# Second layer of a two-layer metaformer: taps summed on VectorE or GpSimd, gates spread by four row tiles, experts by halves in one bank

## The chip, the cores and the metric

The kernel runs on one core of one Trainium2 chip, in one launch. The metric is the device time of that launch in microseconds (us), shown as the median of several runs. A profiled execution gives the span from its first to its last instruction, and this span lies a little below the time of the same run.

## What is computed

All arrays are float32. The input `x` holds 8 images of 128 channels and 32x32 positions, so 1024 tokens of 128 channels for each image. The first layer (softmax attention along rows of the image, then a spectral convolution over the tokens) isn't touched by the change. The second layer is, and this is it, cut to what matters:

```python
# x = x + deformable convolution of the normalised x
offset, mask = conv(x, off_w) + off_b, sigmoid(conv(x, mask_w) + mask_b)
for j in range(3):                                   # three taps in a row of the image
    samp = gather(iy0, ix0) * (1 - wy) * (1 - wx) + ...   # four corners of each sample
    out = out + einsum('bhwc,oc->bohw', samp * mask[:, j][..., None], conv_w[:, :, 0, j])
x = x + out + conv_b
# t = t + mixture of experts of the layer-normalised t: 8 experts, the best two of each token
router_probs = softmax(x @ router_w + router_b)
top_p, top_i = top_k(router_probs, 2); top_p = top_p / sum(top_p)
expert_out = einsum('bnd,edc->bnec', x, expert_w) + expert_b
t = t + einsum('bnk,bnkc->bnc', top_p, take_along_axis(expert_out, top_i))
```

The kernel applies the weights of a tap before the gather, so that the three taps of a token are only scaled and added up after it.

## The kernel before

**Order of the program.** Layer one runs first: attention, then the spectral part, which ends in an inverse transform that is done image by image inside the second layer. The second layer is `DeformAndExperts`. `image` writes down for one image a list of operations, each with an engine (or a choice of two), an assumed cost in us, the operations it follows, and the rooms (buffers) that it takes and gives back. `Plan.order` runs through all 8 lists at once as a small clocked model with these costs and with ranks that favour the earlier image, and emits the instructions in the order in which the model starts them. On the chip each engine works strictly through its own part of that order, and semaphores carry the dependences. An assumed cost therefore changes only the order of the instructions and, where an operation has a choice, its engine.

**One image in the second layer.** `lags` and `waves` (lines 2041 to 2056) build the output of layer one in a PSUM bank named `po`, for even and odd tokens in turn; `take_x2` (L1107) copies it out. `back` and `sum_up` (L1134) turn it to token-major layout, `tok`. A normalisation (`norm`, prefix a) follows, then `channels` (L1073 turns it back), then `mixed` (L1201: 8 matmuls that apply the three taps' weights and the offset and mask filters). The results go to tables in HBM (`write`, L1163 and L1167, issued by SyncE), and GpSimd issues 24 gathers for the image (`fetch`, L1244: 8 tiles of 128 tokens by 3 taps). The landed corners are scaled on ScalarE (L1251) or GpSimd (L1257) and folded on VectorE (`fold`, L1266 and L1267) into `sm`, one partial sum for each tap.

`join_taps` (L1272) then adds up the three taps of four tiles on TensorE: three matmuls of `sm` against the identity, 512 columns each, into one bank. `take_x3` (L1281) adds the bank to `tok` on VectorE, which makes `x3`, the input of the expert part. A second `norm` (prefix b) follows for the whole image; where its argument `edge` is true (first norm of the first image, second norm of the last) the Newton steps of the inverse root may run on VectorE in place of GpSimd. `tokens` (L1073) turns the result to channel-major `tc`.

**Gates and experts.** `gates` makes for each token 8 numbers, six of them zero, and writes them into `padded`, in which two tiles of tokens share one 128-column block (64 columns each). Four transposes (L1541) and a copy (L1548) give `gt`: gates on the partitions, two groups of 64 rows. For each of 8 experts then: `spread` (L1357) copies the expert's gate to all 128 partitions by two matmuls of 64 rows and 512 columns, into two banks `pg`; `gate` (L1365) multiplies 1024 tokens by it on VectorE; `expert` (L1373) does two matmuls of 512 columns into two banks `pe`, where the 8 experts add up. `leave` (L1380 and L1385) adds the bias and `x3`, `take_out` copies, and SyncE stores. There is one pair of banks `pg`, and each spread follows the expert before it, across images too: spread, gate, expert, spread form one chain. Other work of TensorE may be placed between a spread and its expert. PSUM has 8 banks of 512 floats per partition: `po` 2, `pt` 2 (all transposes and small results), `pg` 2, `pe` 2.

## Time and profile before

| quantity | value |
| --- | --- |
| median of 4 runs | 1926.96 us (1924.81 to 1936.13) |
| the profiled execution's own time | 1927.2 us |
| its span | 1925.5 us |
| busy TensorE / VectorE / ScalarE / GpSimd | 1728.8 / 1354.8 / 1075.4 / 1135.6 us |
| second layer, from its first matmul to the end | 1346.4 to 1925.5 us |
| first and last gather issued | 1400.5 and 1822 us |
| first spread of image 0 | 1508.8 us |
| gates of 1024 tokens, L1365 | 64 times, 1221 ns on average |
| tap sums on VectorE, L1281 | 16 times, 689 ns on average |

"Busy" is the time in which an engine has an instruction in work. A float32 matmul of the program appears as two matmul records, each with its own weight load, so the count of records is twice that of the matmuls, and since matmuls are pipelined, the duration of a record is longer than the time after which the next one can start. The time from the start of one group to the start of the next is the better price.

### The profile page before, as it was taken

The page shows a single profiled execution, that of the slowest core. Times are in us where ns is not written, and L with a number is a line of the kernel's source. Part 1 is how long each engine was busy: PE and PEld are TensorE (multiplying, and loading weights), DVE is VectorE, ACT ScalarE, POOL GpSimd, SP SyncE. Part 2 cuts the span into 40 slices and gives each one's busy share as a digit, 9 for nine tenths or more (in the row PEclk, how much of TensorE's full clock was granted, in tenths as well). Part 3 has the DMA queues.
Part 4 walks back from the last instruction along what each step waited for, and adds up shares of the span by engine and source line. Part 5 has one row for each costly group of instructions (what it writes and reads, how often), then busy time and mean ns, then how long its engine had stood idle before and what let it go on. Part 6 is the DMA issues. An engine that isn't in the chain of part 4 may idle for free.

```text
span 1925.5 us, 50111 instructions
## 1 busy us (share of the span) xinstructions
PE 1728.8 (90%) x21452; PEld 1002.6 (52%) x21452; DVE 1354.8 (70%) x2073; ACT 1075.4 (56%) x1724; POOL 1135.6 (59%) x1194
## 2 busy tenths in 40 slices
PE   6899999999999999997577899998976989789876
PEld 3455555555555555554233788887754435343332
DVE  3588788888888888887456666665267878778752
ACT  3667667676767666663335455553246667565610
POOL 3678777777878777784330444443067776667700
PEclk9999999999999999999799999999998899889999
DMA  1000000000000000000877122213598856466500
GB/s 29 13 2 23 2 2 23 2 24 2 24 1 24 2 23 2 2 13 2 188 192 236 53 64 69 68 49 125 151 278 270 240 153 185 145 177 189 159 11 22
DMA packets 157959, 156.03 MB, mean 81 GB/s; under 512 B 15408, under 2 KB 136832, under 8 KB 156320
## 3 DMA queue, kind: packets, MB, share of 16 engines
q1 hardware_dynamic: 142368, 102.41, 18.7%
q0 software_dynamic: 15360, 50.34, 8.4%
q8 instruction: 170, 2.79, 0.6%
q14 instruction: 61, 0.50, 0.1%
HBM read 96.39 MB, written 56.33 MB: 79 GB/s over the span
## 4 chain that ended last, share of the span: by engine, by line
PE 70%; DVE 7%; issue 6%; POOL 5%; ACT 5%; DMA 2%; SPq 1%; ACTq 0%; POOLq 0%; DVEq 0%
PE s L603 14%; PE av L655 12%; PE p_g L1891 6%; PE z L624 6%; PE p_out L1373 5%; PE p_z L1940 5%; PE rb L638 3%; PE p_g L1357 3%; DVE ga L1365 2%; PE p_mix L1201 2%; PE p_x L1272 2%; ACT e L608 2%; PE po L2056 2%; PE pq L558 2%; PE pk L572 2%
## 5 line engine op out<-in xcount | busy, mean ns | idle before, releaser
L617 POOL TENSOR_TENSOR t<-e 128x1024 f32<-128x1024 f32 x256 | 607.8, 2374 | 208.4 <-ACT e L608 208.1
L645 DVE TENSOR_TENSOR e<-e,rb 128x2048 f32<-128x2048 f32 x256 | 570.4, 2278 | 85.4 <-PE rb L638 85.4
L608 ACT ACTIVATE e<-s 128x2048 f32<-128x2048 f32 x256 | 480.9, 1878 | 257.0 <-PE s L603 254.5
L603 PE MATMUL s<-q,k 32*128 32x256 f32 x4096 | 296.9, 404 | 14.4 <-ACT e L608 13.5
L655 PE MATMUL av<-e,vt 128*32 128x256 f32 x4096 | 288.2, 389 | 4.0 <-DVE e L645 2.7
L1244 POOL DMA_INDIRECT g<-tab,idx x192 | 194.1, 1011 | 147.3 <-DMA tab<-hx 70.8
L603 PEld LDWEIGHTS s<-q,k 32*128 32x128 f32 x4096 | 187.0, 186 | 138.7 <-ACT e L608 116.7
L1251 ACT ACTIVATE g<-g,w 128x128 f32<-128x128 f32 x612 | 187.5, 390 | 44.3 <-DMA g<-tab,idx 41.1
L1916 POOL TENSOR_SCALAR at<-uc 128x256 f32<-128x256 f32 (+2 forms) x62 | 75.2, 1215 | 173.6 <-PE p_z L1940 118.7
L655 PEld LDWEIGHTS av<-e,vt 128*32 128x32 f32 x4096 | 101.4, 109 | 141.6 <-issue 84.7
L1891 PE MATMUL p_g<-v,a 32*128 32x128 f32 x4096 | 159.3, 284 | 9.4 <-ACT ga L1623 3.7
L1373 PE MATMUL p_out<-ga,ew 128*128 128x512 f32 x256 | 129.7, 631 | 39.3 <-DVE ga L1365 39.2
L631 DVE RECIPROCAL r<-z 128x256 f32<-128x256 f32 x64 | 112.5, 1757 | 73.4 <-PE z L624 73.2
L1891 PEld LDWEIGHTS p_g<-v,a 32*128 32x128 f32 x4096 | 132.3, 186 | 38.3 <-issue 23.0
L1365 DVE TENSOR_TENSOR ga<-p_g,tc 128x1024 f32<-128x1024 f32 x64 | 78.2, 1221 | 76.0 <-PE p_g L1357 75.9
L624 PE MATMUL z<-t,group 128*32 128x256 f32 x2048 | 122.3, 379 | 0.0
L1625 DVE COPY gb<-p_g 128x512 f32<-128x512 f32 x128 | 82.4, 685 | 46.7 <-PE p_g L1891 46.1
L1625 DVE COPY ga<-p_g 128x512 f32<-128x512 f32 x128 | 82.4, 685 | 44.1 <-PE p_g L1891 44.1
L1623 ACT COPY gb<-p_g 128x512 f32<-128x512 f32 x128 | 68.7, 589 | 69.7 <-PE p_g L1891 68.9
L1623 ACT COPY ga<-p_g 128x512 f32<-128x512 f32 x128 | 68.7, 589 | 66.7 <-PE p_g L1891 66.7
L1373 PEld LDWEIGHTS p_out<-ga,ew 128*128 128x128 f32 x256 | 47.1, 197 | 97.2 <-DVE ga L1365 53.3
L624 PEld LDWEIGHTS z<-t,group 128*32 128x32 f32 x2048 | 66.4, 110 | 44.1 <-issue 0.3
(310 smaller groups left out, 2363.8 us busy)
## 6 DMA issues: line engine op xcount, KB each, us to landing
tab<-hx SPq DMA_DIRECT2D x24, 512.0 KB, 4.6
tab<-hx SPq DMA_DIRECT2D x72, 128.0 KB, 4.7
ud<-us SPq DMA_DIRECT2D x8, 1024.0 KB, 5.3
uc<-ud SPq DMA_DIRECT2D x16, 512.0 KB, 4.1
yd<-zs SPq DMA_DIRECT2D x32, 256.0 KB, 3.3
ga<-yd SPq DMA_DIRECT2D x32, 256.0 KB, 6.3
xc<-in_x SPq DMA_DIRECT2D x8, 512.0 KB, 3.9
x1d<-xt SPq DMA_DIRECT2D x8, 512.0 KB, 2.8
```

The source lines that it names most:

```text
L603: nc.tensor.matmul(s[:, j, c, :], img["k"][rows, hg, 2 * r + c, :], q[rows, qc * QU : (qc + 1) * QU], start=True, stop=True,)
L608: nc.scalar.activation(e.rearrange("p j c q -> p (j c q)"), s.rearrange("p j c q -> p (j c q)"), AF.Exp, scale=float(HD) ** -0.5,)
L617: nc.gpsimd.tensor_add(t, e[:, :, 0, :], e[:, :, 1, :])
L624: nc.tensor.matmul(un["z"][32 * j : 32 * j + 32, 0:QU], group, un["t", r][:, j, :], start=(r == 0), stop=(r == 3), skip_group_check=True,)
L645: nc.vector.tensor_tensor(e, e, un["rb"].unsqueeze(2).to_broadcast([P, NH, 2, QU]), ALU.mult)
L655: nc.tensor.matmul(qrt["av"][32 * j : 32 * j + 32, 0:QU], img["v"][:, 2 * r + c, P * hg + 32 * j : P * hg + 32 * j + 32], un["e", r][:, j, ...
L1244: nc.gpsimd.indirect_dma_start(out=t["g", i][:, tap].rearrange("p k c -> p (k c)"), out_offset=None, in_=rows, in_offset=bass.IndirectOffs ...
L1251: nc.scalar.activation(t["g", i][:, tap, k, :], t["g", i][:, tap, k, :], AF.Identity, scale=t["w"][:, i, tap, k : k + 1],)
L1373: nc.tensor.matmul(t["out"][:, j, :], self.ew[:, e, :], t["xg", e][:, 512 * j : 512 * j + 512], start=(e == 0), stop=False, skip_group_che ...
L1623: self.nc.scalar.copy(dst, src)
L1625: self.nc.vector.tensor_copy(dst, src)
L1891: nc.tensor.matmul(banks[j][:, i * P : (i + 1) * P], self.a[rows, 4 * n + i, :], self.v[rows, ch].rearrange("p f k -> p (f k)"), start=Tru ...
```

## The change

Five things change in the second layer; the two layers compute the same function as before.

- **Taps.** `join_taps` and its three matmuls go. `take_x3` adds the three taps of `sm` and `tok` by three additions of 512 elements, on VectorE or on GpSimd, as the planner places them.
- **Gates.** `padded` gives each of the 8 tiles 32 columns, four tiles to a block of 128, so there are two transposes for an image and `gt` is half as wide. `own`, `eb` and their setup go from two groups of 64 rows to four of 32.
- **Spread and gate.** One `spread` now does four experts for half an image: 16 matmuls of 32 rows and 128 columns, whose four row groups write to four different banks. `gate` multiplies 2048 elements at once. The room `pg` is four banks, `po` one bank in place of two.
- **Experts.** For each half of an image, two groups of four matmuls of 512 columns add up in one bank `pe`. `leave` (now 8 matmuls of 128 columns) comes after the first of the two groups.
- **Last image.** Its second norm and its gates run in two halves. Apart from that the planner's assumed costs change (the transposes from 0.6 to 1.1, `mixed` from 0.55 to 0.85, and others).

```diff
-        "sm": 2, "x3": 3, "tt": 1, "tc": 2, "gate": 2, "xg": 3, "ot": 2,
-        "po": 2, "pt": 2, "pg": 1, "pe": 1,
+        "sm": 2, "x3": 3, "tt": 1, "tc": 2, "gate": 2, "xg": 2, "ot": 2,
+        "po": 1, "pt": 2, "pg": 1, "pe": 1,
...
-        for j in range(2):
+        for q in range(4):
             nc.gpsimd.affine_select(
-                out=self.own, in_=self.own, pattern=[[-1, NE], [0, C]], base=-64 * j,
+                out=self.own, in_=self.own, pattern=[[-1, NE], [0, C]], base=-32 * q,
...
-        for j in range(2):
-            nc.sync.dma_start(self.eb[64 * j : 64 * j + NE, :], expert_b)
+        for q in range(4):
+            nc.sync.dma_start(self.eb[32 * q : 32 * q + NE, q, :], expert_b)
...
     def banks(self, tag, name):
-        return self.ps.tile([P, 2, 512], F32, tag=tag, name=name, bufs=self.ROOMS[tag])
+        return self.ps.tile([P, 4, 512], F32, tag=tag, name=name, bufs=self.ROOMS[tag])
...
+    def norm(self, add, prefix, src, dst, eps, ready, take, parts, edge):
+        if parts == 1:
+            return self.norm_part(add, prefix, src, dst, eps, ready, take, range(NT), edge)
+        first = self.norm_part(
+            add, prefix + "0", src, dst, eps, ready[:1], take, range(0, NT // 2), edge
+        )
+        return first + self.norm_part(
+            add, prefix + "1", src, dst, eps, ready[1:], (), range(NT // 2, NT), edge
+        )
...
-        def join_taps(half):
-            t["px", half] = self.bank("pt", "p_x")
-            for tap in range(TAPS):
-                nc.tensor.matmul(
-                    t["px", half], self.ident, t["sm", half][:, :, tap, :],
-                    start=(tap == 0), stop=(tap == TAPS - 1),
-                )
-        def take_x3(half):
+        def take_x3(half, engine):
...
-            nc.vector.tensor_tensor(
-                flat(t["x3"][:, cols, :]), t["px", half], flat(t["tok"][:, cols, :]), ALU.add
-            )
+            x, sm = t["x3"][:, cols, :], t["sm", half]
+            engine.tensor_tensor(x, sm[:, :, 0], sm[:, :, 1], ALU.add)
+            engine.tensor_tensor(x, x, sm[:, :, 2], ALU.add)
+            engine.tensor_tensor(x, x, t["tok"][:, cols, :], ALU.add)
...
-                q = add(
-                    "PE", 1.9, partial(join_taps, half), [q],
-                    take=("pt",) if half else ("pt", "x3"), give=("sm",),
-                )
                 ready.append(
-                    add("DVE", 0.7, partial(take_x3, half), [q, biased] + ready,
-                        give=("pt", "tok") if half else ("pt",))
+                    add({
+                        "DVE": (2.0, partial(take_x3, half, nc.vector)),
+                        "POOL": (3.5, partial(take_x3, half, nc.gpsimd)),
+                    }, 0, None, [q, biased] + ready, take=() if half else ("x3",),
+                        give=("sm", "tok") if half else ("sm",))
                 )
...
-            ("tt",), b == B - 1,
+            ("tt",), 2 if b == B - 1 else 1, b == B - 1,
...
+        gates = self.gates(add, t, tc, b, 2 if b == B - 1 else 1)
+        def spread(half, first):
+            t["pg"] = self.banks("pg", "p_g")
+            for e in range(4):
+                for q in range(4):
+                    rows = slice(32 * q, 32 * q + 32)
+                    nc.tensor.matmul(
+                        t["pg"][:, q, e * P : (e + 1) * P], self.own[rows, first + e, :],
+                        t["gt"][rows, half, :], start=True, stop=True, skip_group_check=True,
+                    )
+        def gate(half):
...
+            nc.vector.tensor_tensor(
+                t["xg"], t["pg"].rearrange("p q (e n) -> p e q n", e=4),
+                x.unsqueeze(1).to_broadcast([P, 4, 4, P]), ALU.mult,
+            )
+        def experts(half, first):
...
+            for e in range(4):
                 nc.tensor.matmul(
+                    t["out"], self.ew[:, first + e, :], xg[:, e, :],
+                    start=(first + e == 0), stop=(first + e == NE - 1), skip_group_check=True,
+                )
+        def leave(half):
+            for q in range(4):
+                out = t["out"][:, q * P : (q + 1) * P]
                 nc.tensor.matmul(
+                    out, self.eb[:, q, :], t["gt"][:, half, :],
+                    start=False, stop=False, skip_group_check=True,
+                )
                 nc.tensor.matmul(
+                    out, t["x3"][:, half * 4 + q, :], self.ident,
+                    start=False, stop=False, skip_group_check=True,
                 )
...
         for half in range(2):
+            done = []
+            for first in (0, 4):
+                end = half == 1 and first == 4
+                p = add(
+                    "PE", 1.1, partial(spread, half, first), [gates[half], tc[half]] + n,
+                    take=("pg",),
+                )
+                p = add(
+                    "DVE", 2.4, partial(gate, half), [p] + e, take=("xg",),
+                    give=("pg", "tc") if end else ("pg",),
+                )
+                e = [p]
+                q = add(
+                    "PE", 3.8, partial(experts, half, first), [p] + done,
+                    take=() if first else ("pe",), give=("xg",),
+                )
+                done = n = [q]
+                if first == 0:
+                    done = [add(
+                        "PE", 2.1, partial(leave, half), done, give=("x3", "gate") if half else (),
+                    )]
+            q = add(copied(take_out, half), 0, None, [q], take=("ot",), give=("pe",))
...
+    def gates(self, add, t, tc, b, parts):
+        if parts == 1:
+            return self.gates_part(add, t, tc, b, range(NT), "", ("gate",)) * 2
+        half = NT // 2
+        return (
+            self.gates_part(add, t, tc[:1], b, range(0, half), "0", ("gate",))
+            + self.gates_part(add, t, tc[1:], b, range(half, NT), "1", ())
+        )
```

## The prediction

> **What bounds the kernel now.** The change touches only the second layer, so I first cut that layer into three stages with the view that gives each engine's busy time by stretch: A up to the first spread of image 0, B up to the first spread of image 6, C the rest. Columns: stretch, length, busy us of TensorE, weight loads, VectorE, ScalarE, GpSimd, then clock, DMA share, GB/s.
>
> ```profile
> 1338.00:1508.80 170.80, 132.34 (x597) 90.88 (x588) 95.65 (x323) 80.21 (x221) 82.70 (x123) 0.90 0.81 246
> 1508.80:1837.40 328.60, 290.92 (x1003) 136.91 (x1002) 255.48 (x610) 200.53 (x603) 224.64 (x321) 0.96 0.57 169
> 1837.40:1925.50 88.10, 64.66 (x202) 25.46 (x202) 31.57 (x72) 7.25 (x16) 0.00 (x0) 0.97 0.05 17
> ```
>
> In B, TensorE is busy 291 of 329 us (89%), VectorE 78%, GpSimd 68% (with the 0.30 us that it stands after nearly every gather, 143 gathers, some 267 us or 81%). In A the DMA queues carry the load. In C no engine is full, so I read its order of time, TensorE and VectorE:
>
> ```profile
> 1890.42 1.13 PE L1357 MATMUL p_g<-gt,ga 64*128 64x512 f32 x4
> 1892.88 1.98 PE L1373 MATMUL p_out<-ga,ew 128*128 128x512 f32 x4 [1.33 <-DVE ga L1365]
> 1894.80 1.13 PE L1357 MATMUL p_g<-gt,ga 64*128 64x512 f32 x4
> ...
> 1891.60 1.23 DVE L1365 TENSOR_TENSOR ga<-p_g,tc 128x1024 f32<-128x1024 f32 x1 [3.15 <-PE p_g L1357]
> ```
>
> Spread, gate and expert take turns: 1890.42 to 1891.60 to 1892.88 to 1894.80, that is 1.18 + 1.28 + 1.92 = 4.37 us for an expert, and each engine waits for the other. Last, the groups that the change removes, and the rows nearest to what it adds:
>
> ```profile
> L1357 PE MATMUL p_g<-gt,ga 64*128 64x512 f32 x256 | 74.3, 658 | 1.2 <-ACT gt L1548 1.2
> L1272 PE MATMUL p_x<-sm,ident 128*128 128x512 f32 x96 | 47.7, 635 | 3.0 <-DVE tok L1134 1.6 <-ACT hx L1209 1.2
> 1061.97 1.32 PE L1891 MATMUL p_g<-v,a 32*128 32x128 f32 x32 [0.46 <-ACT ga L1623]
> L1281 DVE TENSOR_TENSOR x<-p_x,tok x16: 680/691/692, 1445.8 to 1845.7; 128x512 f32<-128x512 f32 x16
> L1267 DVE TENSOR_TENSOR sm<-g x64: 557/558/5391, 1423.1 to 1840.7; 128x384 f32<-128x384 f32 x64
> 1822.81 5.02 POOL L1257 TENSOR_TENSOR g<-g,w 128x512 f32<-128x512 f32 x5
> 1822.86 5.39 DVE L1267 TENSOR_TENSOR sm<-g 128x384 f32<-128x384 f32 x1
> ```
>
> (Durations with slashes are least/median/greatest ns.) L1891, in layer one, already runs 16 matmuls of 32 rows and 128 columns, 32 records, in 1.32 us: four row groups do overlap. The last two lines matter for the rivals.
>
> **Prices on TensorE**, from start to start. A 512-column matmul: two records at 0.43 = 0.86 us (the weight loads of L1373 follow each other at 0.43). A spread pair: 1.05. A burst as L1891: 1.1 (1.32 less the run-out of the last record). Four 128-column matmuls (L1385): 1.09. One 64-row bias matmul (L1380): 1.05.
> - Spread: 64 pairs x 1.05 = 67.2 become 32 bursts x 1.1 = 35.2: -32.0.
> - Taps: 48 x 0.86 = 41.3 go: -41.3.
> - Experts: 128 matmuls either way: 0.
> - `leave`: per half 1.05 + 1.09 = 2.14 becomes 8 x 0.273 = 2.18: +0.6 over 16 halves. Gate transposes 32 to 16: -4.4.
> Sum -77 us of some 474 that these prices give for the layer before.
>
> **Prices on VectorE.** The new adds have two SBUF operands, 512 elements. From L1267 (384: 0.557) and L1266 (768: 0.95), 512 cost 0.69. The instruction order of the changed kernel puts all 16 `take_x3` on VectorE, none on GpSimd: 48 x 0.69 = 33.1 in place of 11.0, +22. The gate: 512 elements from PSUM 0.69, 1024 1.224, so 2048 are 2.29; 32 x 2.29 = 73.3 against 78.2: -5. The two-part last image repeats about 20 small instructions at 0.2, +4; fewer copies and biases fall to VectorE (`hc` 5 to 2, bias 6 to 4, `gt` 5 to 2), about -8. Sum +13. GpSimd gets 4 more multiplies at 1.05 and 2 more bias adds at 2.36: +9.
>
> **Off the path.** Two more affine selects (1.09 each) stand before the first gather, where GpSimd is idle for 67.7 us; two more 4 KB loads on SyncE at 998 us, over 500 us before use. Uncovered they would be 3 us.
>
> **Stage A.** By the order, the 8 `mixed` of image 0, whose tables release the gathers, no longer alternate with the waves of image 2: TensorE work ahead of them falls from 46.6 to 35.6 us at the prices above. Against that, `po` is one bank: a `lags` of the other parity must wait for `take_x2` (1.07 us, about 1.4 with both hand-overs), three times before the tables, +4. So -7; ends -11 (copies hidden) and +6 (the DMA, at 0.81 of its time, sets A anyway, and later copies wait on ScalarE behind its scaling). I take -6.
>
> **Stage B.** Between the same two spreads the order holds 287 us of TensorE work before and 243 after. VectorE goes from 255 to about 266 (13 adds of 2.07 for 12 of 0.69, less 4 of gates and 4 of copies), GpSimd with gaps from 267 to 276. The gain ends where one of the others fills up. If the fullest engine can be used as TensorE is now (0.885): TensorE 247/0.885 = 279, VectorE 266/0.885 = 301, GpSimd 276/0.885 = 312. So -50, -28 or -17. I take -28, VectorE: each spread hands over to it and back, and it now also holds the adds, while GpSimd's gathers can run ahead as far as the four `g` rooms let them. Behind a waiting gate stand folds and statistics, and for the folds wait the `g` rooms and so the gathers.
>
> **Stage C.** A step of four experts for half an image: 1.4 (burst and hand-over) + 2.34 + 3.63 (two pairs: 1.91 + 1.72) = 7.37. Eight steps 59.0 against 16 x 4.37 = 69.9: -10.9; the taps in it -2.6; four `leave` +0.2. Before, transposes (2.2) and router matmuls (1.9) stood in gaps of 1.28 and showed by 1.5; in gaps of 2.34 they hide: -1.5. But the last image's choices of gates in halves (27 small ops and a copy, 7.8 us) stand on VectorE ahead of one gate and TensorE covers 5.0: +2.8. Sum -12. It may be more: before, image 6's gates came late by the 5.39 us fold above; now its first gate follows the last adds directly. Ends -5 and -20; I take -13.
>
> **Sum** against the profiled execution: 1927.2 (span 1925.5, 1.7 around it) - 6 - 28 - 13 = 1880. That execution lies 0.2 us above the median of 1926.96, so no correction.
>
> **A rule that speaks against the change.** The rows first: the add that goes, L1281, reads PSUM and never took over 692 ns in 16 times; folds with both operands in SBUF took up to 5391, in the one case shown exactly while GpSimd did five multiplies in a row. The three new adds are all of the second kind. On average L1267 and L1266 lie 0.10 and 0.08 above their medians, so 48 adds pay 5 us, which the range covers. The Trainium skill, "SBUF — State Buffer", section "SBUF: two separate sides", says the same as a rule: VectorE and GpSimd share one pair of ports as an exclusive lock, held for the whole instruction, and a VectorE instruction with two SBUF inputs needs it against a GpSimd one that reads SBUF. By that rule alone an add that meets one multiply waits about 1 us; an estimate from it, all 48 meeting one, would be some 50 us, and no gain.
>
> **Rivals.**
> 1. *TensorE stays the bound* and the others give way: A -9, B -42 (its 44 us of work less 2 of longer uncovered gates), C -16: 1860. For it: nearly all `spread` to `experts` gaps in B hold 1.4 us or more of other work. Against it: VectorE then stands at 266/287 = 93%.
> 2. *The gathers set B.* GpSimd stands after most gathers, and between the images it waited 6.0 and 8.7 us for statistics. Then B gives 0 to -17, with C -13 and A 0: 1897 to 1914, say 1906.
> 3. *Slower: the adds meet GpSimd.* Place: `take_x3` in A and B, in front of gates. Price: 48 x s for a mean stall s. At s = 0.98 the 47 us are eaten; at 1.5, 1927 - 47 + 72 = 1952. For it: the 5.39 us row. Against it: median folds take 558 ns, so most don't meet.
> 4. *The row groups don't overlap in this place.* 16 x 0.273 = 4.4 for a burst, +3.3 x 32 = 105: 1985. L1891 speaks against it.
>
> **Numbers.** Chances: forecast 0.50, rival 1 0.22, rival 2 0.18, rival 3 0.08, rival 4 0.02. The time is the forecast's, 1880; its own parts give 1927 - (9 + 42 + 20) = 1856 and, with 6, -10 and -5, 1918. As a range I take 1853 to 1908, which leaves out rivals 3 and 4, the worse half of rival 2 and a little of rival 1. A measurement of this kernel tells 0.5% (10 us) from no change. Faster 0.87, same 0.04 (the end of rival 2 and mild stalls of rival 3), slower 0.09.
>
> **What would show it.** Right: no matmul reads `sm`; the new spreads take 1.1 to 1.4 us in 32 records; the gate about 2.29 us; in the last stage a gate every 7.4 us, or 9.6 where a `leave` stands between; VectorE over 85% busy between the first spreads of images 0 and 6, in about 300 us. Wrong: adds far above 0.69 us, above all beside GpSimd multiplies (rival 3); that stage above 320 us with GpSimd full (rival 2) or below 290 (rival 1); the first gather after 1400 us.

## The result, and the profile after

| | before | after |
| --- | --- | --- |
| median of the comparison | 1927.45 us (63 runs) | 1923.58 us (42 runs) |
| ratio, 95% interval | | 0.9976 [0.9968, 0.9984] |
| span of the profiled execution | 1925.5 us | 1921.0 us |
| first matmul of layer two to first spread (A) | 162.4 us | 149.2 us |
| to the first spread of image 6 (B) | 328.6 us | 343.6 us |
| to the end (C) | 88.1 us | 83.1 us |
| first and last gather issued | 1400.5, 1821.8 us | 1394.4, 1825.8 us |

A starts here at the first `po` matmul (1346.4 before, 1345.1 after); B ends and C starts at the first spread of image 6, the last image but one. The kernel is faster by 4 us, not by 47: the sign was right and the size far off. A gained 13 us and B lost 15; A and B together took 491.0 us before and take 492.8 now. C gained 5. So the sign comes from C and from an earlier start of the layer by 1.3 us; stage B, which was to bring 28 of the 47, went the other way.

The same view of the three stages, after (stretch, length, busy us of TensorE, weight loads, VectorE, ScalarE and GpSimd, granted clock, DMA share, GB/s; in lines of the profile PE is TensorE, PEld its weight loads, DVE VectorE, ACT ScalarE, POOL GpSimd and SP SyncE):

```profile
1345.10:1494.30 149.20, 119.27 (x436) 80.94 (x436) 84.98 (x286) 70.94 (x193) 77.11 (x113) 0.86 0.77 231
1494.30:1837.90 343.60, 269.46 (x1623) 166.71 (x1622) 287.98 (x670) 210.68 (x626) 250.80 (x337) 0.85 0.58 175
1837.90:1921.00 83.10, 57.99 (x398) 32.67 (x398) 32.31 (x77) 4.87 (x12) 0.00 (x0) 0.84 0.04 13
```

TensorE's busy time in B fell by 21 us though the list of work fell by 44; its clock fell from 0.96 to 0.85. VectorE is at 84%, no engine is full. The durations that the forecast rested on came out nearly as priced (the gate at 2.28 for 2.29 us, the adds at 0.69 to 0.82 for 0.69), in the groups of VectorE:

```profile
L1378 DVE TENSOR_TENSOR ga<-p_g,tc 128x2048 f32<-128x2048 f32 x32 | 73.1, 2283 | 53.7 <-PE p_g L1369 53.7
L1294 DVE TENSOR_TENSOR x<-x,sm 128x512 f32<-128x512 f32 x16 | 13.1, 816 | 0.5
L1293 DVE TENSOR_TENSOR x<-sm 128x512 f32<-128x512 f32 x16 | 12.1, 758 | 0.3
L1295 DVE TENSOR_TENSOR x<-x,tok 128x512 f32<-128x512 f32 x16 | 11.1, 692 | 0.5
```

**The stretch of the gathers.** B begins and ends at spreads. GpSimd's own stretch, from the first gather to the last, reads otherwise, first before, then after:

```profile
1400.50:1822.80 422.30, 359.50 (x1250) 183.03 (x1250) 321.07 (x837) 259.57 (x782) 302.32 (x438) 0.94 0.67 201
1394.40:1826.80 432.40, 338.03 (x1857) 213.85 (x1856) 346.83 (x854) 264.22 (x784) 321.11 (x444) 0.85 0.65 197
```

GpSimd is busy for 302 us before, and gaps of at most 0.30 us ahead of its instructions (longer ones counted as 0.30) add 76: 90% of 422. After it is 321 + 74, or 91% of 432. Counted the same way, TensorE goes from 88% to 81% and VectorE from 84% to 86%. GpSimd's work grew by 19 us where the forecast had 9; 8.5 of them are the same 192 gathers, which take longer (line, engine, operation, count, busy us, mean ns, idle time before them), one line of each kernel:

```profile
L1244 POOL DMA_INDIRECT g<-tab,idx x192 | 194.1, 1011 | 147.3 <-DMA tab<-hx 70.8 <-issue 48.4 <-DVE sm L1267 8.4
```

```profile
L1263 POOL DMA_INDIRECT g<-tab,idx x192 | 202.6, 1055 | 94.5 <-issue 48.2 <-DMA tab<-hx 15.6 <-DVE a_st L1019 12.5
```

The chain of waits, asked for that stretch (1394 to 1826 us), gives shares by engine and line. Before:

```profile
by line: PE p_out L1373 16.6%; PE p_g L1357 9.4%; PE p_x L1272 7.0%; PE p_mix L1201 6.9%; DMA g<-tab,idx 6.4%; issue 5.8%; DVE ga L1365 4.5%; POOL g L1244 3.8%; PE po L2056 3.2%; DVE g L1266 2.9%; SPq L1167 2.3%; ACT tt L1035 2.2%; PE p_l L
```

After:

```profile
by line: POOL g L1263 13.8%; issue 10.8%; DMA g<-tab,idx 7.9%; DVE g L1285 5.7%; DVE ga L1378 4.4%; PE p_out L1388 4.0%; ACT g L1270 3.5%; POOL g L1276 3.2%; PE p_mix L1220 3.2%; ACT ht L1052 2.2%; DVE sm L1286 1.8%; ACT tt L1052 1.5%; DVE 
```

Added up over all its pieces, TensorE had 233 of the 432 us of this chain before and has 53 now; VectorE went from 60 to 136, GpSimd from 41 to 114. The change did take TensorE off most of the chain, and two engines that were nearly as full took its place at the same length. Whether either of them sets that length the chain alone doesn't show; the experiments ask.

**Stage C.** TensorE, in order of time (start, duration, group, idle time before it and what ended it), and the clock in the same stretch:

```profile
1871.08 1.17 PE L1369 MATMUL p_g<-gt,ga 32*128 32x128 f32 x32
1874.67 5.15 PE L1388 MATMUL p_out<-ga,ew 128*128 128x512 f32 x8 [2.41 <-DVE ga L1378]
1879.75 1.17 PE L1369 MATMUL p_g<-gt,ga 32*128 32x128 f32 x32
1883.43 5.37 PE L1388 MATMUL p_out<-ga,ew 128*128 128x512 f32 x8 [2.51 <-DVE ga L1378]
...
1903.10 3.67 PE L1388 MATMUL p_out<-ga,ew 128*128 128x512 f32 x8 [2.50 <-DVE ga L1378]
```

```profile
1867.40:1874.20 6.80, 4.86 (x53) 3.50 (x51) 1.88 (x1) 0.00 (x0) 0.00 (x0) 1.00 0.00 0
1874.20:1877.60 3.40, 2.93 (x4) 1.38 (x5) 0.42 (x1) 0.00 (x0) 0.00 (x0) 0.50 0.00 0
1877.60:1884.50 6.90, 4.39 (x40) 2.28 (x40) 2.29 (x1) 0.58 (x1) 0.00 (x0) 0.99 0.10 38
1884.50:1887.90 3.40, 3.40 (x6) 1.34 (x5) 0.00 (x0) 0.00 (x0) 0.00 (x0) 0.51 0.00 0
```

The spread takes 1.17 us in 32 records, as forecast. But the step is 1879.75 - 1871.08 = 8.67 us, not 7.37: after most of the gaps at a gate the clock is granted at half for 3.4 us, just when four experts run. Of the eight groups of the stage six take 5.2 to 5.8 us in place of 3.63. Two stay near the forecast: one that had other work before it, and the one at 1903.10, after a gap of 2.50 us like the others.

What tells that gap from the others is its place. All changes of the granted clock in the traces of this case lie on one grid of 3.41 us. Two steps of that grid with the clock at full (TensorE, weight loads and VectorE busy, then the clock):

```profile
1870.80:1874.21 3.41, 1.46 (x36) 1.14 (x34) 1.89 (x1) 0.00 (x0) 0.00 (x0) 1.00 0.00 0
1901.52:1904.93 3.41, 1.83 (x5) 0.90 (x6) 1.44 (x1) 0.00 (x0) 0.00 (x0) 1.00 0.05 19
```

In the first TensorE stood for 1.95 us, and the next step had half the clock; in the second the end of a gap that began in the step before left 1.58 us, and the clock stayed. Over the second layer in all 20 traces, 319 of the 320 full-clock steps in which TensorE stood for 2.0 us or more were followed by half clock, and 28 of some 1750 in which it stood for less than 1.0 us; between the two it was mixed.

### The profile page after: what moved, and what is told of

Its sections match the earlier page's. It is cut to its first block, busy times and chain, and to the rows that moved or that the text cites. A ratio compares the mean times of both kernels' runs of the same rounds, so it can differ in the third digit from the quotient of the medians.

```text
span 1921.0 us, 51642 instructions
## 1 busy us (share of the span) xinstructions
PE 1689.6 (88%) x22204; PEld 1031.3 (54%) x22204; DVE 1378.7 (72%) x2102; ACT 1074.5 (56%) x1716; POOL 1158.4 (60%) x1202
## 4 chain that ended last, share of the span: by engine, by line
PE 59%; DVE 11%; POOL 9%; issue 7%; ACT 5%; DMA 3%; SPq 2%; POOLq 0%; DVEq 0%; ACTq 0%
PE s L603 14%; PE av L655 12%; PE p_g L1926 6%; PE z L624 6%; PE p_z L1975 5%; PE rb L638 3%; POOL g L1263 3%; PE p_out L1388 3%; DVE ga L1378 2%; DMA g<-tab,idx 2%; ACT e L608 2%; PE pk L572 2%; PE pq L558 2%; DVE g L1285 1%; DVE zs L1987 1%
## 5 line engine op out<-in xcount | busy, mean ns | idle before, releaser
L1263 POOL DMA_INDIRECT g<-tab,idx x192 | 202.6, 1055 | 94.5 <-issue 48.2
L1388 PE MATMUL p_out<-ga,ew 128*128 128x512 f32 x256 | 144.3, 716 | 50.9 <-DVE ga L1378 49.2
L1388 PEld LDWEIGHTS p_out<-ga,ew 128*128 128x128 f32 x256 | 56.7, 231 | 122.1 <-issue 82.7
L1378 DVE TENSOR_TENSOR ga<-p_g,tc 128x2048 f32<-128x2048 f32 x32 | 73.1, 2283 | 53.7 <-PE p_g L1369 53.7
```

Source lines behind the costliest of these rows:

```text
L1263: nc.gpsimd.indirect_dma_start(out=t["g", i][:, tap].rearrange("p k c -> p (k c)"), out_offset=None, in_=rows, in_offset=bass.IndirectOffs ...
L1388: nc.tensor.matmul(t["out"], self.ew[:, first + e, :], xg[:, e, :], start=(first + e == 0), stop=(first + e == NE - 1), skip_group_check=True,
```

## The experiments

Three theories were set against each other for B: (1) the chain of spread, gate and experts on TensorE and VectorE, with its cold clock; (2) VectorE is full; (3) GpSimd's gathers set the pace. Four batches fell on chips on which the kernel before takes 1951 to 1952 us, and the last on one like the first (1924 us). Only runs of one kind of chip are compared with each other; ratios are to the kernel before on the same chip. A + B and C are from one profiled execution of each run, and its time can lie off the median: it was 4.8 us under it in r_after, 4.4 under in a_gate and 13.3 under in a_fetch, 6.1 over in e3_taps_only. Differences of A + B or B below some 10 us are therefore no more than hints.

| run | median us | ratio [95%] | A + B | C |
| --- | --- | --- | --- | --- |
| r_before | 1952.3 | 0.9999 [0.9982, 1.0016] | 518.1 | 88.1 |
| r_after | 1972.5 | 1.0117 [1.0077, 1.0157] | 537.5 | 85.4 |
| e1_warm_tail | 1958.8 | 1.0046 [1.0021, 1.0071] | 534.0 | 74.3 |
| e1_warm_all | 1964.2 | 1.0065 [1.0043, 1.0088] | 545.5 | 75.2 |
| e2_taps_back | 1994.3 | 1.0220 [1.0181, 1.0259] | 568.4 | 81.7 |
| e3_taps_only | 1963.0 | 1.0057 [1.0035, 1.0078] | 527.0 | 93.6 |
| e4_two_experts | 1971.4 | 1.0097 [1.0068, 1.0127] | 541.3 | 85.6 |
| a_experts | 1934.0 | 0.9933 [0.9904, 0.9963] | 518.7 | 71.0 |
| a_gate | 1943.9 | 0.9961 [0.9945, 0.9976] | 523.0 | 69.9 |
| a_adds | 1966.4 | 1.0082 [1.0051, 1.0113] | 533.2 | 83.7 |
| a_fetch | 1925.0 | 0.9874 [0.9845, 0.9903] | 496.4 | 72.0 |
| e5_ahead | 1928.2 | 0.9889 [0.9857, 0.9921] | 521.2 | 61.3 |
| e6_one_room | 1943.4 | 0.9964 [0.9939, 0.9989] | 524.2 | 73.0 |
| e7_before_po1 | 1953.0 | 1.0008 [0.9989, 1.0026] | 516.8 | 88.6 |
| e8_old_costs | 1974.6 | 1.0118 [1.0077, 1.0160] | 546.7 | 83.2 |
| e9_cold_cost | 1978.3 | 1.0139 [1.0097, 1.0180] | 550.6 | 78.5 |
| e10_scale_act (chip like the first) | 1907.0 | 0.9903 [0.9885, 0.9921] | 482.6 | 80.1 |
| e11_ahead_act (chip like the first) | 1907.7 | 0.9898 [0.9880, 0.9916] | 495.9 | 65.2 |

### The two kernels on the other chips

> The changed kernel as it is, beside the three that follow, so that they are compared on one chip. As profiled before: stage A (first matmul of layer two to the first spread) 149 us, stage B (to the first spread of the last image) 344 us, stage C (to the end) 83 us.

> The kernel before as it is, for its stages on these chips, where it takes 1951 us and the changed kernel 1972 us (A 153.3, B 384.2, C 85.4). On the chip of the first comparison it had A 162.4, B 328.6, C 88.1. If the 22 us by which the changed kernel is slower here lie in the late signals of TensorE that its trace shows from the first gather on, B of before is about 353 and its trace shows fewer such delays; if they lie in the change itself, A and C differ as well.

No edit. Here the changed kernel is slower than before by 1.2%. B grew from 352.6 to 384.2 us (+32, where the first chip had +15); A (165.5 to 153.3) and C (88.1 to 85.4) moved about as on the first chip. These traces show what the first chip's don't, TensorE's signals arriving late (start, duration, engine, group, idle time before and its end, where "remote" and "issue" mean that the profile names no sender; r_after):

```profile
1569.12 1.17 PE L1369 MATMUL p_g<-gt,ga 32*128 32x128 f32 x32
1570.22 1.65 PE L1220 MATMUL p_mix<-gw,hc 128*128 128x411 f32 x4
1577.93 2.29 DVE L1378 TENSOR_TENSOR ga<-p_g,tc 128x2048 f32<-128x2048 f32 x1 [5.51 <-remote]
1578.02 0.91 ACT L1228 COPY hx<-p_mix 128x411 f32<-128x411 f32 x2 [6.64 <-issue]
```

The spread is recorded as done at 1570.3, and both the gate and the copy of another matmul's result start together 7.6 us later. Of 15 gates between 1490 and 1840 us before which VectorE was idle, 10 came more than half a microsecond after the end of their spread, some 50 us in all; on the first chip it was none of 9. The expectation for r_before held on B (353) but not on the signals: summed from the end of a matmul that should signal to the next signal seen, its trace has 123 us of such time and r_after's 130. The late signals burden both kernels; how much of the 32 us is theirs is not told apart. Nor does the trace tell whether the signal or the matmul itself was late.

The two stages B, r_before and then r_after:

```profile
1512.20:1864.80 352.60, 300.79 (x1001) 139.43 (x1000) 249.97 (x610) 201.02 (x603) 222.89 (x321) 0.92 0.54 157
```

```profile
1496.40:1880.60 384.20, 284.00 (x1623) 172.54 (x1622) 282.81 (x672) 209.07 (x623) 247.17 (x333) 0.82 0.53 157
```

TensorE is busy for 17 us less, VectorE for 33 and GpSimd for 24 more, and no engine passes 74% in the second: the stage is longer without a fuller engine.

### The clock

```diff
         def experts(half, first):
+            for _ in range(2 if b >= B - 2 else 0):
+                nc.tensor.matmul(
+                    t["out"], self.idle, self.ew[:, 0:4, :].rearrange("p e c -> p (e c)"),
+                    start=(first == 0), stop=False, skip_group_check=True,
+                )
             for e in range(4):
```

`idle` holds zeros, so the two matmuls add nothing; they fill the gap at the gate. e1_warm_all has `True` as its condition.

> The changed kernel, and for the last two images two more matmuls of 512 columns with a zero stationary ahead of each group of four experts (they add zero to the output bank); the order of all other instructions is unchanged. Theory (clock): in the changed kernel TensorE stands 2.4 us in each gate of the last stage, the granted clock falls to half again and again (0.84 on average from the first spread of image 6 on, 0.97 before the change), and four experts take 5.2 us in place of 3.6. The two matmuls (1.7 us warm) fill the wait: clock of the last stage to 0.95 or more, experts near 3.6 us, the last stage from 83 to about 73 us, the whole 8 to 10 us below the changed kernel. Rival (the serial hand-over alone costs the time): clock as before or without effect, last stage 83 us or longer by what of the two matmuls does not fit in the wait.

> The same two zero matmuls ahead of every group of four experts, all images. Theory (clock): the middle stage too loses some 40 us to half clock (0.85 on average over 344 us); with the fillers its clock rises towards 0.95, it shortens by 10 to 25 us although TensorE gets 24 x 1.7 = 41 us of extra work, most of it in waits; whole 15 to 35 us below the changed kernel. Rival (VectorE and the order of the program set the middle stage, the half clock is only a sign of waiting): middle stage unchanged or longer by up to 20 us, only the last stage gains its 8 to 10.

More matmuls in the last two images made C 11 us shorter than in r_after, with the clock up:

```profile
1880.60:1966.00 85.40, 61.42 (x398) 33.81 (x398) 31.27 (x75) 4.87 (x12) 0.00 (x0) 0.81 0.04 13
```

```profile
1881.10:1955.40 74.30, 64.03 (x430) 34.83 (x430) 31.27 (x75) 4.87 (x12) 0.00 (x0) 0.97 0.04 15
```

The first line is r_after, the second e1_warm_tail. That the cold clock costs C its gain is shown. In B the fillers of e1_warm_all bring the clock only to 0.86 from 0.82, and B is 7.5 us longer, as the rival in its expectation had it. They add matmuls there too, and the clock of before was 0.92 on these chips, so what the cold clock costs B stays open.

### Taking work away

In this order: a_experts, a_gate (its experts then read the two products that are left), a_adds and a_fetch (tap 1 then uses the rows of tap 2). Each leaves work out, so it no longer computes the layer.

```diff
-            for e in range(4):
+            for e in (0, 3):
...
-                t["xg"], t["pg"].rearrange("p q (e n) -> p e q n", e=4),
-                x.unsqueeze(1).to_broadcast([P, 4, 4, P]), ALU.mult,
+                t["xg"][:, 0:2], t["pg"].rearrange("p q (e n) -> p e q n", e=4)[:, 0:2],
+                x.unsqueeze(1).to_broadcast([P, 2, 4, P]), ALU.mult,
...
-            engine.tensor_tensor(x, sm[:, :, 0], sm[:, :, 1], ALU.add)
-            engine.tensor_tensor(x, x, sm[:, :, 2], ALU.add)
-            engine.tensor_tensor(x, x, t["tok"][:, cols, :], ALU.add)
+            engine.tensor_tensor(x, sm[:, :, 0], t["tok"][:, cols, :], ALU.add)
...
+            if tap == 1:
+                return
             rows = self.tabs[b % 2][tap].rearrange("r s c -> r (s c)")
```

> Two of the four expert matmuls of each group are left out (experts 1, 2, 5 and 6 add nothing); the order of the work is unchanged. A group loses 1.8 us of TensorE at full clock and about 2.6 us at the clock seen there. Theory 1, the chain spread-gate-experts on TensorE and VectorE sets stage B too: 24 groups fall away 44 to 63 us, time -50. Theory 2, VectorE is the fullest engine and sets stage B (288 busy of 343.6): stage B loses under 10 us, stage C 5 to 10. Theory 3, GpSimd's gathers set stage B (251 busy and 36 of gaps between gathers): the same, under 10 us in B.

> Each gate multiplies 1024 of its 2048 elements (experts 2, 3, 6 and 7 take the gated values of 0, 1, 4 and 5); the order is unchanged. A gate takes 1.15 us in place of 2.28, 27 us in the 24 gates of stage B and 4.5 in stage C. Theory 1 (chain): B -27 or more, since TensorE idles less and its clock rises; theory 2 (VectorE full): B about -27; theory 3 (gathers): B under -10.

> Two of the three adds that join the taps are left out (tap 0 alone is added to the tokens); the order may shift a little. VectorE loses 2 x 0.8 us per half image, 19 us in the six images of stage B. Theory 1 (chain of spread, gate, experts; the adds are outside it): B under -6. Theory 2 (VectorE full): B about -19. Theory 3 (gathers): B under -6.

> The changed kernel without the 64 gathers of tap 1 (its products are made from tap 2's rows); every other instruction stays. GpSimd loses 48 x 1.36 us = 65 us of stage B (1.06 busy and 0.3 between two gathers), the transfers a third of the gathers' bytes. Theory 3 (GpSimd's gathers set B): B -40 to -65. Theory 1 (the chain spread, gate, experts on TensorE and VectorE): B under -10. If TensorE's late signals on these chips come from the gathers, they get rarer and B loses a third of the 40 us by which it is longer here, -13.

B was 384.2 us. Of the work taken from it, it gave back 17 of 43 to 62 us of experts (24 groups at 1.8 to 2.6), 12 of 27 of gates, 3 of 20 of adds, 29 of 65 of gathers: a third, not quite a half, a sixth, not quite a half, each give or take the 5 to 13 us by which the profiled executions lie off their medians. With fewer gathers the late signals became fewer too (60 us in place of 130), so part of the 29 may be theirs. Each of the three theories wanted nearly all of at least one. VectorE alone (theory 2) falls with the adds; the chain alone and the gathers alone fall too. On the first kind of chip these four were not run.

C fell by 14 and 16 us with halved experts and gates, but also by 13 in a_fetch, which leaves C's spreads, gates and experts as they are. There the clock of C is 0.97, and only one of its groups is slow, after gaps like those of the changed kernel:

```profile
1838.10:1910.10 72.00, 51.40 (x411) 30.80 (x410) 32.28 (x90) 8.27 (x19) 2.97 (x3) 0.97 0.05 19
1875.76 3.67 PE L1390 MATMUL p_out<-ga,ew 128*128 128x512 f32 x8 [2.50 <-DVE ga L1380]
1884.73 5.40 PE L1390 MATMUL p_out<-ga,ew 128*128 128x512 f32 x8 [2.41 <-DVE ga L1380]
```

So the same rhythm can meet a warm or a cold clock, and that alone moves C: the eight groups of experts take 31 us here and 43 in r_after, 12 of the 13 us.

### Parts alone, and the same instructions in other orders

e2_taps_back is the changed kernel with `join_taps` and the `take_x3` of before (assumed cost 2.6), e3_taps_only the kernel before with the `take_x3` of the change. The other three are e7_before_po1 from before, e8_old_costs and e9_cold_cost from after. One line of each is shown; e8 gives the other transposes, `mixed` and the scaling of the norms their costs of before as well:

```diff
-        "po": 2, "pt": 2, "pg": 1, "pe": 1,
+        "po": 1, "pt": 2, "pg": 1, "pe": 1,
...
-                "PE", 1.1, partial(back, half), parts + [p] * half, take=("pt",) if half else ("pt", "tok"),
+                "PE", 0.6, partial(back, half), parts + [p] * half, take=("pt",) if half else ("pt", "tok"),
...
-                    "PE", 3.8, partial(experts, half, first), [p] + done,
+                    "PE", 5.2, partial(experts, half, first), [p] + done,
```

> The changed kernel with the three taps added on TensorE again, as in the kernel before (cost given to the planner 2.6). If the adds on VectorE are what eats the gain (VectorE busy 288 of 344 us in the middle stage), this gets faster than the changed kernel, by 5 to 25 us, with VectorE below 80% there. If TensorE work still counts and the clock is the trouble, the 41 us that come back also fill waits and keep the clock up: between 5 us faster and 15 us slower than the changed kernel, clock above 0.9. If neither, and TensorE is simply the bound, 20 to 40 us slower.

> The kernel before with only the three adds in place of the joining matmuls; spread, gates and experts as before. TensorE -41 us, VectorE +22 us. With the rest of the change in place the adds were worth 22 us (taps put back: 1994 against 1972.5). If the gain is independent of the rest: 1951 - 22 = 1929, the best so far here, and the rest of the change costs 43. If the taps gain only because the changed kernel has one bank less for them (pt and po): no gain, 1945 to 1951.

> The kernel before with one po bank in place of two. The prediction gave this 4 us in stage A and nothing in B. Beside before on this chip (A 165.5, B 352.6, C 88.1, 1952 us): A +4, B within 5, 1956. If the single bank is what lengthens B in the changed kernel (352.6 to 384.2), B is 370 or more.

> The changed kernel with the assumed costs of before for the transposes (0.6 in place of 1.1), mixed (0.55 for 0.85) and the scaling in the norms (1.6 for 1.8): the same instructions in another order. If the order that the planner makes is a matter of little weight, B stays at 384 within 5 and the time at 1972 within 6. If the order carries much of stage B, it moves by 10 us or more, either way.

> The changed kernel with an assumed cost of 5.2 for four experts in place of 3.8, which is what they take at the clock of its stage C: the same instructions in another order. As for the old costs: within 5 us of 384 in B if the order weighs little; 10 us or more, either way, if it carries much of B. If the planner only lacked the true cost, it gets shorter.

The parts don't add up. The taps alone cost 11 us (1952 to 1963), the rest alone 42 (to 1994), both together 20. Beside the rest, then, taking the 41 us of taps off TensorE gained 22 (e2 against r_after), as its last expectation had it for TensorE's own work; alone it lost 11. In e3 what TensorE then waited for can be read between 1515 and 1860 us (what waited, for what, us in total, times, longest):

```profile
PE p_gt L1533 <- DVE tok L1134: 37.6, 2, 22.4
```

Twice TensorE stood, for 22.4 and 15.2 us, at a transposing of gates, with all its later work queued behind it. The gates themselves were ready: in the first case VectorE had written them at 1559.2 us, 15.7 before the wait ended. What was missing was a `pt` bank, which VectorE's `sum_up` (L1134) emptied late, behind other work and the new adds. With before's taps on TensorE the longest wait of that kind was 6.4 us (r_before).

One `po` bank makes A 4.4 us longer (165.5 to 169.9), about the +4 of the forecast, and nothing that shows in the time. e8 and e9 ask whether the order alone matters. With the old costs B is 384.0 us as in r_after, A is 9.4 longer, and the time is 1974.6 for 1972.5, within the intervals: its first expectation held, that the order weighs little. With the dearer experts B is 10.5 longer and the time 1978.3; these intervals overlap too. So the order was not shown to carry B, and the true cost of the experts didn't make the planner's order better.

### Spreads ahead of the experts, and smaller groups

e4_two_experts only makes the groups two experts (`first` in 0, 2, 4, 6). e5_ahead does that and changes the rooms, the row tiles and what a spread follows; e6_one_room is e5_ahead with `po` 2 and `pg` 1:

```diff
-        "po": 1, "pt": 2, "pg": 1, "pe": 1,
+        "po": 1, "pt": 2, "pg": 2, "pe": 1,
...
-        return self.ps.tile([P, 4, 512], F32, tag=tag, name=name, bufs=self.ROOMS[tag])
+        return self.ps.tile([P, 2, 512], F32, tag=tag, name=name, bufs=self.ROOMS[tag])
...
+            for e in range(2):
+                for j in range(2):
+                    rows = slice(64 * j, 64 * j + 64)
+                    nc.tensor.matmul(
+                        t["pg", half, first][:, j, e * 256 : (e + 1) * 256],
+                        self.own[rows, first + e, :], t["gt"][rows, half, :],
+                        start=True, stop=True, skip_group_check=True,
+                    )
...
-                    "PE", 1.1, partial(spread, half, first), [gates[half], tc[half]] + n,
+                    "PE", 1.05, partial(spread, half, first), [gates[half], tc[half]] + n[-2],
```

Here `n[-2]` are the experts two groups back.

> The changed kernel with groups of two experts in place of four: 8 spread matmuls, a gate of 1024 elements, two expert matmuls, 8 groups an image. Theory (clock): the wait for a gate falls from 2.4 to 1.3 us as in the kernel before, the clock of the last stage returns to 0.95 or more, a step takes 0.8 + 1.3 + 1.9 = 4.0 us for two experts of half an image in place of 8.7 for four; last stage about 72 us plus nothing, whole 10 to 30 us below the changed kernel. Rival (the middle stage is set by VectorE and by the order): last stage gains under 10 us, the middle stage does not move, the whole 0 to 10 us below.

> The changed kernel with groups of two experts over half an image, spread by two row tiles of 64 into two banks, and two such rooms: the spreads of two groups are issued ahead of the experts of the first, so a gate of 1.2 us lies beside the next spread and beside experts. Theory 1 (the chain of spread, gate and experts on two engines is what costs): four experts take 2.1 + 0.2 + 3.6 = 5.9 us of TensorE in place of 8.7 to 9.4; C 85 to 73, its clock up to 0.95, and B -10 to -25: total 1940 to 1955. Rival (TensorE's own work is what costs): 22 us more spread in B, B longer by 5 to 10, C -5.

> e5_ahead (A 152.4, B 368.8, C 61.3, 1928 us) with one pair of banks for spreads in place of two, and the freed banks given to po: spread, gate and experts take turns again, in groups of two experts over half an image. If issuing spreads ahead is what e5_ahead gained: a step of two experts in C takes 1.2 + 1.3 + 1.8 = 4.3 us in place of 2.95, C about 80, B back to 380 and the time near 1965. If the smaller groups and 64-row tiles did it: C 61 to 65, B 369, time 1928 to 1932.

Smaller groups alone (e4) gain nothing: C is 85.6 us for 85.4, though its clock is 0.90 for 0.81. e5_ahead is 44 us faster than r_after and 24 faster than before, more than expected; C is 61.3 us at a clock of 0.99:

```profile
1496.40:1865.20 368.80, 286.76 (x1201) 171.76 (x1200) 290.45 (x712) 208.29 (x622) 239.61 (x333) 0.87 0.56 163
1865.20:1926.50 61.30, 54.31 (x256) 31.63 (x256) 31.33 (x81) 5.77 (x13) 3.81 (x3) 0.99 0.05 18
```

So theory 1 holds for C: with a gate beside the next spread, TensorE hardly waits there and doesn't cool. Taking the second room away gives back 15 of the 44 us, 12 of them in C, between what its two expectations had. So spreading ahead is worth about 15, if the second `po` bank that e6 also gets changes as little as e7 suggests. What the other 29 come from (64-row tiles, two-bank rooms, smaller groups, another order) isn't told apart.

### GpSimd relieved

```diff
                 s.append(add({
                     "ACT": (1.57, partial(scale, i, tap)),
-                    "POOL": (1.1, partial(multiply, i, tap, nc.gpsimd)),
                 }, 0, None, [d, w_ready]))
```

> The changed kernel with all corners scaled on ScalarE and none on GpSimd (39 multiplies of 1.06 us while gathers run, some 41 us, become 61 us on ScalarE, which is busy for 264 of 432 us there). Theory 3, GpSimd's stream of gathers sets the pace: from first to last gather 470 us (changed kernel on these chips) becomes 430 to 450, the time 1972 becomes 1935 to 1952. Rival, the stretch is set by the orders of all engines together and by none alone, or ScalarE takes GpSimd's place: within 8 us of 1972.

> The same on e5_ahead (1928 us, from first to last gather 456 us): with theory 3 the stretch becomes 416 to 436 and the time 1890 to 1908; with the rival within 8 us of 1928.

On a chip like the first, e10 takes 1907 us against 1924, a ratio of 0.9903 where the changed kernel had 0.9976. The expected stretch has to be read from that chip's 432 us: theory 3 wanted 392 to 412, and a time of 1887 to 1904; the rival wanted 1916 to 1932. The time fell between the two, the stretch stayed with the rival.

```profile
1392.10:1818.70 426.60, 324.88 (x1859) 207.25 (x1859) 333.08 (x863) 294.45 (x911) 263.17 (x407) 0.86 0.68 200
```

GpSimd's busy time there fell by 58 us (more than the multiplies' 41) and the stretch by 6. The other gains are 2 us at its start and 7 after its end. So GpSimd's fullness was not the one bound either, although with its short gaps it went from 91% to 79% of the stretch. ScalarE, which took the multiplies, is at 69%. The chain now spreads over all (gathers 11.4%, table writes issued by SyncE 8.6%, and so on):

```profile
by line: POOL g L1263 11.4%; issue 10.6%; SPq L1186 8.6%; DMA g<-tab,idx 6.4%; ACT g L1270 5.6%; PE p_out L1387 5.5%; DVE ga L1377 4.4%; DVE g L1285 4.3%; PE p_mix L1220 3.8%; DMA tab<-hx 2.8%; PE p_g L1368 2.7%; ACT tt L1052 1.7%; PE po L2
```

e11 adds nothing on this chip: its C is 15 us shorter, its A + B 13 longer. Its expectation can't be judged, since e5_ahead was not run on a chip of this kind. Both beat the kernel before by more than the changed kernel did on the first chip, and e5_ahead beats both kernels on the others.

## Why the prediction was wrong, point by point

- **The failed step is in stage B:** "The gain ends where one of the others fills up", with three ends of its own (-50, -28, -17), of which it took VectorE's -28. What the runs showed in its place: B grew by 15 us, A + B moved by +1.8, and no engine filled up (VectorE at 84% of B in 344 us, where 88.5% in 301 was forecast). Its own largest term was GpSimd's 312 us. It set that aside because the gathers "can run ahead", and it had read GpSimd at 81% over a stretch that begins and ends at spreads (143 gathers, where the trace has 138, and no other short gaps; with all of them it is 85%). Over the gathers' own stretch GpSimd stood at 90%, TensorE at 88%. By that count there was little room to begin with, and GpSimd's own work grew by 19 us in place of 9. But that GpSimd took the place isn't shown: relieved of 58 us it gave back 6. Rival 2 came nearest, at 1906, and missed as well: 1923.6 lies above its 1914, and above the 1918 to which the forecast's own worst ends add up; neither let B grow. The sign came out right without this step.
- **The rule behind it failed too.** It supposed that one engine binds and that the next can be filled to 0.885. The runs that took work away, on the slower kind of chip, show a stage in which every engine pays back a sixth to a half of what was taken, and putting the 41 us of taps back on TensorE cost 22. On the first kind e10 shows the same for GpSimd, which gave back a tenth. Such a stage has no single fullest engine whose filling ends the gain.
- **Stage A:** -13 for -6, with the first gather at 1394.4 us, 6 us earlier. But an earlier first spread was no gain of its own: B was longer by as much and 2 us more.
- **Stage C:** -5 for -13. The mechanism was right and one term mis-sized: the experts at 3.63 us were a price at full clock. At 5.2 to 5.4 us a step takes 8.67, not 7.37. e1_warm_tail has 3.70 us and the forecast's gain (88.1 to 74.3), a_fetch at 0.97 has 72.0.
- **TensorE:** its list in B fell by 44 us at full-clock prices, but its busy time only by 21. The granted clock stood at half for 102 us of B, where before it was 26 (171 and 64 in all of layer two, the sums of the clock's records). The sum held no term for it; how much of the missing 23 us it explains was not measured. The Trainium skill, "TensorE: Matmul & The Clock Gate", section "Why this matters for your kernels", asks for no idle gaps over some 3 us; here shorter gaps, of 2.41 and 2.51 us, were enough when most of one lay in one step of the 3.41 us grid, and the same gaps in a_fetch mostly were not. Before, gaps of 1.33 us, once in 4.37, left the clock at 0.97.
- **VectorE:** +24 us over the layer (381.3 to 405.3) for +13: the adds took 36.3 for 33.1, the gate 73.1 for 73.3. The 8 us of copies and biases left it as forecast; all other instructions together took some 12 us more, for 4 forecast.
- **Rivals 3 and 4 are out.** The adds' means lie at most 0.12 us above 0.69, 3 us in all, and the row groups overlap. The Trainium skill's rule on the shared ports ("SBUF — State Buffer", section "SBUF: two separate sides"), taken for all 48 adds, gave an estimate of some 50 us; the longest add took 2.68 us, but the medians are 0.69, so few met anything.

What stays open: what holds A + B at its length once no engine is above 91% even of the gathers' stretch. Shown is that no single engine's work does: on the slower chips for TensorE, VectorE and GpSimd, on the first kind for GpSimd alone. The order of the queues and the cold clock in B are left as candidates; neither was settled.

## What to carry to other kernels

Before crediting a bottleneck's relief, put every engine's busy time, with its short gaps, over its own stretch of work. Where three of them lie within a few per cent, as at 90, 88 and 84% here, expect only a part of any relief back: a sixth to a half here, and 6 of 58 us for the fullest. A sum that divides the fullest engine's work by a share can then miss by the whole of its term. Price matmuls with the clock that the new rhythm may get: in stage C a longer wait at each turn cost nearly all that the merged work saved (8.67 us a step, where two steps of 4.37 stood before), and issuing the next turn's work ahead removed both the wait and the cold clock. Judge a planner's order by the sum over stages, because an earlier start of one can be given back in the next.

## What was not expected of the hardware

In four of the five batches the kernel before took 24 us longer than on the first chip (1951 against 1927 us), with equal times up to the first matmul of layer two (1346.8 and 1346.4 us). At the gates of r_after TensorE's signals reached VectorE up to 7.6 us after the recorded end of the matmul. Such delays came in bursts, only between the first and the last gather; on the first chip none was above 0.6 us. With a third of the gathers gone (a_fetch) the unsignalled time in the trace fell from 130 to 60 us, so the gathers seem to have a part in it; how was not tried. A gather's issue by GpSimd took 1011 ns in before, 1055 in after, 1028 in r_after and 1040 in e10_scale_act, for the same 192; why isn't shown.
